# Running sums of an attention kernel: merge by transfer into two rings, numerators copied by VectorE, lent buffers placed by when they come free

## The chip, the cores and the metric

The kernel runs on one core of a Trainium2 chip. The metric is device time in microseconds (us), from the first to the last instruction of the core and what lies around it, as a median of several runs. Lower is better.

## The reference, cut to what matters

Two layers follow each other on an input of 4 x 256 x 48 x 48. Each normalizes its input in groups, computes and adds the result to the input. The first layer is a 3x3 convolution with batch norm and ReLU, then attention over all 2304 positions with 8 heads of 32 channels, then a projection. The second layer builds dynamic filters and a last batch norm. The change touches only the attention of the first layer:

```python
q, k, v = (qkv[:, :, :d], qkv[:, :, d:2 * d], qkv[:, :, 2 * d:])
attn = jax.nn.softmax(jnp.einsum('bhdn,bhdm->bhnm', q, k) * scale, axis=-1)
out = jnp.einsum('bhem,bhnm->bhen', v, attn).reshape(B, C, H, W)
out = jnp.einsum('oc,bchw->bohw', proj_w, out) + proj_b[None, :, None, None]
```

The kernel computes the softmax without subtracting the maximum: numerators (exponentials times v) and denominators (sums of exponentials over the keys) are built apart and divided at the end.

## The kernel before

The four batches run one after the other. For each, an attention stage (`attention`) is followed by a stage (`dynamic_filters`) that does the second layer of this batch, with the convolution and the q, k, v products of the next batch woven in by a planner that keeps a clock of estimated costs. The attention stage itself has no planner: its order is the order of the loop.

**Units and steps.** A unit is 512 queries of one group of four heads. Eight units cover 2048 queries of the two groups; the ninth (`last`) takes the remaining 256 queries of both groups. Each unit runs over 18 tiles of 128 keys, so a batch has 162 steps (u, m), in `steps`.

**One step.** `scores` issues the matmuls of the four heads (line 1331) into PSUM: head 0 into the tile `so` (one bank, one buffer), heads 1 to 3 into `se` (three banks, two buffers, which denominators and projections use as well, by `three`). ScalarE takes the exponentials (line 1339 for head 0, line 1340 for the rest) into a buffer `p` of 128 x 4 x 512 values, one of four that are used in rotation. One step later `weigh` multiplies p with v (line 1365) into the PSUM tile `num` (one buffer), and VectorE adds p to the running sum `acc` (line 1380).

**Lending.** From unit 1 on, at m = 2, 5, 8, 11 and 14 (`LENT`; the last unit leaves the fifth out), VectorE adds head 0 only. The other three heads are written by a transfer from GpSimd's queue into `extra`, a part of the weight ring: the first as a plain copy (line 1382), the others as accumulating transfers (line 1384). Each must wait for the one before it, because they accumulate in the same place. The buffer p is lent until the transfer has read it.

**End of a unit.** After m = 17, VectorE adds `extra` to `acc` (line 1387) and ScalarE copies the numerators from PSUM to `ao` (line 1390), which frees `num` for the next unit. The closing of the unit (`close`) comes later, at m = 1 of the unit after the next: matmuls with ones sum `acc` over the keys of a tile (line 1396), VectorE turns the result by two transposes and a reciprocal (lines 1408 to 1411) and multiplies the numerators (line 1418). In the last unit, unit 6 is closed at m = 1, unit 7 at m = 2, and the last itself at the end of the stage. There the sums over p, acc and extra are taken by matmuls alone.

**The last unit's two halves** share one `num` tile. To start it, four matmuls with a tile of zeros (line 1362) clear the bank ahead of the first products.

**Projections.** At m = 6 of units 3, 5, 7 and of the last unit one chunk (two in unit 7) of 384 columns is projected (`project`, line 1454) and added to the residual by VectorE (line 1463); SP stores it.

**The weight ring.** It has 3072 values per partition. `taken(t)` loads the weights of the next batch's convolution into it on SP's queue, a third at a time; `taken(0)` uses the last third. Before, `extra` is the first half of the ring, and `taken(0)` is issued ahead of the attention stage. `following[0]` (`opened`), called after the last step, starts the next convolution's sums on GpSimd and issues `taken(1)`.

Of the kernel before, what the change touches and what calls it, by code (L numbers as in the profile page):

```python
# [8 lines left out]
F32 = mybir.dt.float32  # L9
F32R = mybir.dt.float32r  # L10
AF = mybir.ActivationFunctionType
ALU = mybir.AluOpType
# [5 lines left out]
P = 128  # L18
NH = C // P
HEADS = 8  # L20
D = C // HEADS
# [4 lines left out]
NT = N // P  # L26
# [7 lines left out]
QC = 512  # L34
SAFE = 60.0
LENT = (2, 5, 8, 11, 14)
NEVER = float("inf")
LATE = (4, 3)
AHEAD = 2500.0
# [18 lines left out]
def conv_preact_kernel(  # L58
# [12 lines left out]
    nc = tc.nc  # L71
# [480 lines left out]
    with tc.tile_pool(name="w", bufs=1) as wpool, tc.tile_pool(  # L552
        name="act", bufs=1
# [14 lines left out]
        ring = wpool.tile([P, 3 * 1024], F32, tag="ring", name="ring")  # L568
# [735 lines left out]
        def attention(b, q, k_, vT, pools, spare, project, scratch, following):  # L1304


            ps_s, ps_a, work0 = pools
            ao = keep("h", f"ao_{b}")
            zeros = work0.tile([P, D], F32, tag="zeros", name=f"zeros_{b}", bufs=1)
            nc.gpsimd.memset(zeros, 0.0)  # L1310

            extra = scratch.rearrange("p (j n) -> p j n", j=3)
            scratch = work0.tile([P, QC], F32, tag="rt", name=f"rt_{b}", bufs=1)

            whole, rest = N // QC * QC, N % QC
            units = [[(g, q0, QC, 0)] for q0 in range(0, whole, QC) for g in range(NH)]
            units.append([(g, whole, rest, g * rest) for g in range(NH)])
            assert NH * rest == QC
            heads = [slice(j * D, (j + 1) * D) for j in range(4)]

            def three(name):
                return ps_s.tile([P, 3, 512], F32, tag="s", name=name)

            def scores(u, m):
                s1, s3 = ps_a.tile([P, 512], F32, tag="one", name=f"so_{b}_{u}_{m}"), three(f"se_{b}_{u}_{m}")
                for g, q0, n, at in units[u]:
                    for j, r in enumerate(heads):
                        dst = s3[:, j - 1] if j else s1  # L1330
                        nc.tensor.matmul(  # L1331
                            dst[:, at : at + n],
                            k_[r, g, m * P : (m + 1) * P],
                            q[r, g, q0 : q0 + n],
                            start=True,
                            stop=True,
                        )
                p = work0.tile([P, 4, QC], F32, tag="p", name=f"p_{b}_{u}_{m}", bufs=4)
                nc.scalar.activation(p[:, 0, :], s1, AF.Exp, scale=QS)  # L1339
                nc.scalar.activation(p[:, 1:, :], s3, AF.Exp, scale=QS)  # L1340
                return p

            state = {}
            last = len(units) - 1

            def weigh(u, m, p):
                if m == 0:
                    state[u] = dict(
                        num=ps_a.tile([P, 512], F32, tag="num", name=f"num_{b}_{u}"),
                        acc=work0.tile([P, 4, QC], F32, tag="acc", name=f"acc_{b}_{u}"),  # L1350
                    )
                st = state[u]
                several, end = len(units[u]) > 1, u == last
                if end and m >= NT - 2:
                    sums(u, p, m == NT - 2, m == NT - 1)
                    if m == NT - 2:
                        sums(u, st["acc"], False, False)
                        sums(u, extra, False, False, 1)
                if several and m == 0:

                    for j, r in enumerate(heads):
                        nc.tensor.matmul(st["num"][r, :], zeros, p[:, j, :], start=True, stop=False)
                for i, (g, q0, n, at) in enumerate(units[u]):
                    for j, r in enumerate(heads):
                        nc.tensor.matmul(  # L1365
                            st["num"][r, at : at + n],
                            vT[:, m, g * P + j * D : g * P + (j + 1) * D],
                            p[:, j, at : at + n],
                            start=(m == 0 and not several),
                            stop=(m == NT - 1 and i == len(units[u]) - 1),  # L1370
                        )
                if end and m >= NT - 2:
                    return
                if m == 0:
                    st["first"] = p
                else:
                    other = st["first"] if m == 1 else st["acc"]
                    lend = u > 0 and m in LENT[: len(LENT) - end]
                    js = slice(0, 1 if lend else 4)
                    nc.vector.tensor_tensor(st["acc"][:, js], other[:, js], p[:, js], ALU.add)  # L1380
                    if lend and m == LENT[0]:
                        nc.gpsimd.dma_start(out=extra, in_=p[:, 1:])  # L1382
                    elif lend:
                        nc.gpsimd.dma_start(out=extra, in_=p[:, 1:], accum_op=ALU.add)  # L1384
                if u and m == NT - 1 and not end:
                    rest = st["acc"][:, 1:]
                    nc.vector.tensor_tensor(rest, rest, extra, ALU.add)
                if m == NT - 1 and not end:
                    g, q0, n, _ = units[u][0]
                    nc.scalar.copy(ao[:, g, q0 : q0 + n], st["num"])  # L1390

            def sums(u, rhs, start, stop, first=0):
                if start:
                    state[u]["den"] = three(f"den_{b}_{u}")[:, 0, :]
                for j, r in enumerate(heads[first:]):
                    nc.tensor.matmul(
                        state[u]["den"][r, :], ones, rhs[:, j, :], start=start, stop=stop
                    )

            def close(u):  # L1400

                if u < last:
                    sums(u, state[u]["acc"], True, True)
                else:
                    busy(ps_a.tile([P, 512], F32, tag="one", name="warm"), 5)
                st = state.pop(u)
                t = scratch
                nc.vector.transpose(t, st["den"])
                rc = work0.tile([P, QC // D], F32, tag="rc", name=f"rc_{b}_{u}")
                nc.vector.reciprocal(rc, t.rearrange("p (k d) -> p k d", d=D)[:, :, 0])  # L1410
                nc.vector.transpose(
                    t.rearrange("p (k d) -> p k d", d=D),
                    rc.unsqueeze(2).to_broadcast([P, QC // D, D]),
                )
                for g, q0, n, at in units[u]:
                    dst = ao[:, g, q0 : q0 + n]
                    src = dst if u < last else st["num"][:, at : at + n]
                    nc.vector.tensor_tensor(dst, src, t[:, at : at + n], ALU.mult)

            steps = [(u, m) for u in range(len(units)) for m in range(NT)]  # L1420
            prev = None
            chunk = 0
            for i, (u, m) in enumerate(steps):
                ps = scores(u, m)


                if m == 1 and u > 1:
                    close(u - 2)
                if prev is not None:
                    weigh(*steps[i - 1], prev)  # L1430
                prev = ps
                if m == 2 and u == last:
                    close(u - 1)
                if m == 6 and (u % NH == 1 or u == last):
                    while (chunk + 1) * CH <= units[u if u == last else u - 1][0][1]:
                        pp = three(f"pp_{b}_{chunk}")
                        pp = [pp[:, o] for o in range(NH)]
                        if spare:
                            spare.pop(0)()
                        project(chunk, ao, pp)  # L1440
                        chunk += 1
            assert not spare
            weigh(*steps[-1], prev)
            following[0]()
            close(last)
            following[1]()
            return ao, chunk
# [918 lines left out]
        for b in range(B + 1):  # L2366
# [171 lines left out]
            if b == B - 1:  # L2538
# [1 line left out]
                    out=pads[B % 2].rearrange("p h r w -> p (h r w)")[:, : NH * (2 + NF) * CH],  # L2540
                    in_=late_d[0].rearrange("p m c -> p (m c)"),
                )
            scratch = ring[:, : 3 * QC]
            spare = []
            following = [lambda: None] * 2
            clear(pads[b % 2] if b else pads[1])
            if b + 1 < B:
                load_pad(b + 1)
                us[0] = taken(0)

                def opened(b=b):
                    coming.append(Blocks(b + 1, pads[(b + 1) % 2]))
                    coming[-1].stage0()
                    us[1] = taken(1)
# [97 lines left out]
```

## Time and profile before

| | |
|---|---|
| median of three runs | 2724.35 us (2721.27, 2724.35, 2724.39) |
| the profiled execution | 2722.09 us, of which the span is 2720.2 us |
| mean granted TensorE clock | 0.989 |
| busy: TensorE, VectorE, ScalarE, GpSimd | 2607.0, 2082.2, 1806.3, 809.3 us |
| exponentials, lines 1339 and 1340 | 648 each, 599 and 1449 ns |
| first to last start of line 1339, by batch | 152.4 to 516.6, 807.8 to 1175.6, 1470.0 to 1838.9, 2108.9 to 2477.3 us |
| running-sum adds, line 1380, on all four heads and on one | 412 of 2291 ns, 156 of 692 ns (36 first ones, 2285 ns) |
| merges, line 1387 | 28 of 1758 ns |
| numerator copies, line 1390 | 32 of 593 ns |
| lends, lines 1382 and 1384 | 32 and 124 |

A line of the profile names the source line, the engine, the operation, what it writes and reads, and the shape. In a timeline the first two columns are the start and the duration in us. Brackets at the end of a line give how long the engine had been idle and what ended that. TensorE appears twice: PE is the matmul, PEld the load of the stationary operand. Matmul ends are modelled, so start times are the safer reading. The time from one start of line 1339 to the next is one step of the attention stage.

### The profile page before, as it was taken

The page shows a single profiled execution, that of the slowest core. Times are in us where ns is not written, and L with a number is a line of the kernel's source. Part 1 is how long each engine was busy: PE and PEld are TensorE (multiplying, and loading weights), DVE is VectorE, ACT ScalarE, POOL GpSimd, SP SyncE. Part 2 cuts the span into 40 slices and gives each one's busy share as a digit, 9 for nine tenths or more (in the row PEclk, how much of TensorE's full clock was granted, in tenths as well). Part 3 has the DMA queues.
Part 4 walks back from the last instruction along what each step waited for, and adds up shares of the span by engine and source line. Part 5 has one row for each costly group of instructions (what it writes and reads, how often), then busy time and mean ns, then how long its engine had stood idle before and what let it go on. Part 6 is the DMA issues. An engine that isn't in the chain of part 4 may idle for free. (4 is left out here: it accounts for less than half of the span.)

```text
span 2720.2 us, 42536 instructions
## 1 busy us (share of the span) xinstructions
PE 2607.0 (96%) x16938; PEld 1102.1 (41%) x16938; DVE 2082.2 (77%) x2029; ACT 1806.3 (66%) x2287; POOL 809.3 (30%) x885
## 2 busy tenths in 40 slices
PE   6999999999999999999999999999989999999996
PEld 5632222555562222355555222245546222235554
DVE  7768888757739898857774988885775888885676
ACT  4479888734449898854445888884444888875344
POOL 5200100477520010067750000007775000100453
PEclk9999999999999999999999999999999999999998
DMA  4805445323252445423324354452324444432456
GB/s 174 223 13 105 108 98 110 90 60 108 65 104 58 99 95 108 99 74 87 94 63 84 76 105 99 94 111 75 84 73 120 107 100 99 99 88 72 121 165 219
DMA packets 136942, 273.67 MB, mean 101 GB/s; under 512 B 58024, under 2 KB 98384, under 8 KB 135712
## 3 DMA queue, kind: packets, MB, share of 16 engines
q0 software_dynamic: 26256, 137.71, 22.1%
q1 hardware_dynamic: 110480, 133.17, 18.3%
q8 instruction: 135, 2.21, 0.3%
q14 instruction: 71, 0.58, 0.1%
HBM read 112.12 MB, written 36.04 MB: 54 GB/s over the span
## 5 line engine op out<-in xcount | busy, mean ns | idle before, releaser
L1380 DVE TENSOR_TENSOR acc<-acc,p 128x2048 f32<-128x2048 f32 (+1 forms) x568 | 1052.0, 1852 | 121.0 <-ACT p L1340 71.6
L1340 ACT ACTIVATE p<-se 128x1536 f32<-128x1536 f32 x648 | 938.7, 1449 | 0.0
L1331 PE MATMUL so<-q,k 32*128 32x512 f32 (+1 forms) x1440 | 729.1, 594 | 18.5 <-ACT p L1339 15.9
L1331 PE MATMUL se<-q,k 32*128 32x512 f32 (+1 forms) x4320 | 737.8, 594 | 0.0
L1365 PE MATMUL num<-p,vT 128*32 128x512 f32 (+1 forms) x5760 | 711.9, 561 | 2.2 <-ACT ao L1390 2.2
L1339 ACT ACTIVATE p<-so 128x512 f32<-128x512 f32 x648 | 388.4, 599 | 195.2 <-PE se L1331 89.0
L1331 PEld LDWEIGHTS so<-q,k 32*128 32x128 f32 x1440 | 216.7, 183 | 535.6 <-ACT p L1339 492.0
L1834 POOL TENSOR_TENSOR near<-near,prod 128x384 f32<-128x384 f32 x352 | 353.3, 1037 | 255.3 <-DVE prod L1828 246.4
L1384 POOL DMA_DIRECT2D ring<-p x124 | 105.5, 851 | 776.4 <-ACT p L1340 481.4
L1365 PEld LDWEIGHTS num<-p,vT 128*32 128x32 f32 x5760 | 137.1, 108 | 480.2 <-issue 449.7
L1828 DVE TENSOR_TENSOR prod<-wb,pad 128x768 f32<-128x768 f32 x192 | 181.9, 953 | 84.6 <-ACT wb L1815 51.8
L1331 PEld LDWEIGHTS se<-q,k 32*128 32x128 f32 x4320 | 227.3, 183 | 5.1 <-ACT p L1340 4.1
L1815 ACT COPY wb<-ws 128x384 f32<-128x384 f32 x216 | 108.5, 506 | 166.0 <-DVE prod L1828 129.0
L1382 POOL DMA_DIRECT2D ring<-p x32 | 17.9, 559 | 632.2 <-ACT p L1340 485.1
L1992 PE MATMUL py<-far,wsc 128*128 128x384 f32 x512 | 169.9, 487 | 0.0
L1536 PE MATMUL pg<-pad,wcat 128*45 128x384 f32 x864 | 146.7, 490 | 8.5 <-ACT lg L1594 8.5
L1255 PE MATMUL pq<-hid,wqkv 128*128 128x384 f32 x384 | 133.1, 501 | 15.0 <-ACT hid L1125 12.8
L1504 ACT COPY far<-far 128x512 f32<-128x512 f32 x86 | 90.2, 1108 | 81.1 <-PE far L1762 77.8
L1992 PEld LDWEIGHTS py<-far,wsc 128*128 128x128 f32 x512 | 96.2, 190 | 66.0 <-issue 1.8
L1255 PEld LDWEIGHTS pq<-hid,wqkv 128*128 128x128 f32 x384 | 73.1, 194 | 69.2 <-ACT hid L1125 15.1
L1380 DVE TENSOR_TENSOR acc<-p,p 128x2048 f32<-128x2048 f32 x36 | 82.2, 2285 | 20.8 <-ACT p L1340 14.6
L1736 DVE COPY_PREDICATED amat<-along_y,bmat 128x768 f32<-128x768 uint32 x72 | 92.0, 1277 | 2.4
(334 smaller groups left out, 2865.1 us busy)
## 6 DMA issues: line engine op xcount, KB each, us to landing
ring<-p POOLq DMA_DIRECT2D x156, 768.0 KB, 5.7
ws<-w_d SPq DMA_DIRECT2D x216, 192.0 KB
ring<-u_d SPq DMA_DIRECT2D x36, 512.0 KB
pad<-in_x SPq DMA_DIRECT2D x14, 1152.0 KB
xst<-in_x POOLq DMA_DIRECT2D x36, 192.0 KB, 3.7
x_d<-pad SPq DMA_DIRECT2D x36, 192.0 KB
u_d<-pad SPq DMA_DIRECT2D x12, 512.0 KB
y_d<-y SPq DMA_DIRECT2D x13, 384.0 KB
```

The lines of the kernel that those rows point to most:

```text
L1255: nc.tensor.matmul(pq[:, :CH], wqkv[:, i, s, g * P : (g + 1) * P], hid[:, i, cols], start=(i == 0), stop=(i == NH - 1),)
L1331: nc.tensor.matmul(dst[:, at : at + n], k_[r, g, m * P : (m + 1) * P], q[r, g, q0 : q0 + n], start=True, stop=True,)
L1339: nc.scalar.activation(p[:, 0, :], s1, AF.Exp, scale=QS)
L1340: nc.scalar.activation(p[:, 1:, :], s3, AF.Exp, scale=QS)
L1365: nc.tensor.matmul(st["num"][r, at : at + n], vT[:, m, g * P + j * D : g * P + (j + 1) * D], p[:, j, at : at + n], start=(m == 0 and not s ...
L1380: nc.vector.tensor_tensor(st["acc"][:, js], other[:, js], p[:, js], ALU.add)
L1384: nc.gpsimd.dma_start(out=extra, in_=p[:, 1:], accum_op=ALU.add)
L1536: nc.tensor.matmul(pg[64 * s : 64 * s + NG, :CH], wcat[:, ii, k, :], shifted(ii, cc, k // 3 - 1, k % 3 - 1), start=(i == 0 and k == 0), st ...
L1815: nc.scalar.copy(pw[:, :CH], fetched[c, k][0])
L1828: nc.vector.tensor_tensor(prod.rearrange("p h (r w) -> p h r w", w=WW), wb, src, ALU.mult)
L1834: nc.gpsimd.tensor_tensor(cat[:, h], cat[:, h], prod[:, h], ALU.add)
L1992: nc.tensor.matmul(py[c][:, o, :CH], wsc[:, n * NH + i, o * P : (o + 1) * P], rhs, start=(n == 0 and i == 0), stop=(n == order[-1] and i = ...
```

## The change

1. **Numerators.** VectorE copies `num` to `ao` in place of ScalarE, for all units but the last. The copy is issued in `weigh` at m = 17, ahead of the running-sum add of that step.
2. **Two rings.** `extra` is now two halves of the weight ring, used by units in turn.
3. **Merge.** At the end of a unit an accumulating transfer from GpSimd's queue adds heads 1 to 3 of `acc` into `extra`, and the denominator matmuls read them there. Only unit 7 keeps VectorE's add.
4. **Unit 0 lends too**, at m = 9 and 14 (`FIRST`).
5. **Placement of p.** The four buffers are no longer used in rotation. Each step takes the buffer that is expected to be free first, where a lent buffer counts as held for 5 steps and another for 3 (`until`, `home`).
6. **Zero products** and the tile of zeros are gone: the first half of the last unit starts the bank, the second half does not.
7. **Moved:** in the last unit the closing of unit 7 from m = 2 to 4 and the projection from m = 6 to 8; `taken(0)` from ahead of the attention stage into `opened`, behind its last step.

```diff
 LENT = (2, 5, 8, 11, 14)
+FIRST = (9, 14)
...
-            zeros = work0.tile([P, D], F32, tag="zeros", name=f"zeros_{b}", bufs=1)
-            nc.gpsimd.memset(zeros, 0.0)
-
-            extra = scratch.rearrange("p (j n) -> p j n", j=3)
+
+            extra = scratch.rearrange("p (s j n) -> p s j n", s=2, j=3)
...
+            last = len(units) - 1
+            steps = [(u, m) for u in range(len(units)) for m in range(NT)]
+
+            def lends(u):
+                return FIRST if not u else LENT[:-1] if u == last else LENT
+
+            until, home = [0] * 4, {}
+            for i, (u, m) in enumerate(steps):
+                home[u, m] = until.index(min(until))
+                until[home[u, m]] = i + (5 if m in lends(u) else 3)
...
-                p = work0.tile([P, 4, QC], F32, tag="p", name=f"p_{b}_{u}_{m}", bufs=4)
+                p = work0.tile(
+                    [P, 4, QC], F32, tag=f"p{home[u, m]}", name=f"p_{b}_{u}_{m}", bufs=1
+                )
...
-                if several and m == 0:
-
-                    for j, r in enumerate(heads):
-                        nc.tensor.matmul(st["num"][r, :], zeros, p[:, j, :], start=True, stop=False)
...
-                            start=(m == 0 and not several),
+                            start=(m == 0 and i == 0),
...
+                if m == NT - 1:
+                    g, q0, n, _ = units[u][0]
+                    nc.vector.tensor_copy(ao[:, g, q0 : q0 + n], st["num"])
...
-                    lend = u > 0 and m in LENT[: len(LENT) - end]
+                    lend = m in lends(u)
...
-                    if lend and m == LENT[0]:
-                        nc.gpsimd.dma_start(out=extra, in_=p[:, 1:])
+                    if lend and m == lends(u)[0]:
+                        nc.gpsimd.dma_start(out=extra[:, u % 2], in_=p[:, 1:])
                     elif lend:
-                        nc.gpsimd.dma_start(out=extra, in_=p[:, 1:], accum_op=ALU.add)
-                if u and m == NT - 1 and not end:
+                        nc.gpsimd.dma_start(
+                            out=extra[:, u % 2], in_=p[:, 1:], accum_op=ALU.add
+                        )
+                if m == NT - 1 and not end:
                     rest = st["acc"][:, 1:]
-                    nc.vector.tensor_tensor(rest, rest, extra, ALU.add)
-                if m == NT - 1 and not end:
-                    g, q0, n, _ = units[u][0]
-                    nc.scalar.copy(ao[:, g, q0 : q0 + n], st["num"])
+                    if u == last - 1:
+                        nc.vector.tensor_tensor(rest, rest, extra[:, u % 2], ALU.add)
+                    else:
+                        nc.gpsimd.dma_start(out=extra[:, u % 2], in_=rest, accum_op=ALU.add)
+                        rest = extra[:, u % 2]
+                    st["parts"] = [st["acc"][:, 0], *(rest[:, j] for j in range(3))]
...
-                    sums(u, state[u]["acc"], True, True)
+                    sums(u, state[u]["parts"], True, True)
...
-                if m == 2 and u == last:
+                if m == 4 and u == last:
                     close(u - 1)
-                if m == 6 and (u % NH == 1 or u == last):
+                if m == (8 if u == last else 6) and (u % NH == 1 or u == last):
...
-            scratch = ring[:, : 3 * QC]
+            scratch = ring[:, : 6 * QC]
...
-                us[0] = taken(0)

                 def opened(b=b):
+                    us[0] = taken(0)
                     coming.append(Blocks(b + 1, pads[(b + 1) % 2]))
```

More of the change, by code (lines that the diff above doesn't have):

```diff
@@ L1343, in attention @@
             state = {}
-            last = len(units) - 1
             def weigh(u, m, p):
@@ L1352, in weigh @@
                 st = state[u]
-                several, end = len(units[u]) > 1, u == last
+                end = u == last
                 if end and m >= NT - 2:
@@ L1357, in weigh @@
                         sums(u, st["acc"], False, False)
-                        sums(u, extra, False, False, 1)
-                if several and m == 0:
-                    for j, r in enumerate(heads):
-                        nc.tensor.matmul(st["num"][r, :], zeros, p[:, j, :], start=True, stop=False)
+                        sums(u, extra[:, u % 2], False, False, 1)
                 for i, (g, q0, n, at) in enumerate(units[u]):
@@ L1396, in sums @@
                     nc.tensor.matmul(
-                        state[u]["den"][r, :], ones, rhs[:, j, :], start=start, stop=stop
+                        state[u]["den"][r, :], ones, rhs[j] if type(rhs) is list else rhs[:, j],
+                        start=start, stop=stop,
                     )
@@ L1418, in close @@
                     nc.vector.tensor_tensor(dst, src, t[:, at : at + n], ALU.mult)
-            steps = [(u, m) for u in range(len(units)) for m in range(NT)]
             prev = None
```

## The prediction

> **What bounds the kernel now.** I read first the table of waits, then timelines. The edits lie in the attention stage, and there the exponentials (ScalarE, lines 1339 and 1340) and the matmuls (TensorE, lines 1331 and 1365) run in turn. The waits of the former (total us, times, longest):
>
> ```profile
> ACT p L1339 <- PE se L1331: 89.0, 163, 5.5
> ACT p L1339 <- DMA ring<-p: 23.9, 25, 2.3
> ACT p L1339 <- DVE acc L1380: 10.9, 22, 1.5
> ```
>
> A quiet step on TensorE (start, duration; each product is issued twice, so scores and numerators are two passes each):
>
> ```profile
> 240.15 1.07 PE L1365 MATMUL num<-p,vT 128*32 128x512 f32 x8
> 241.15 0.69 PE L1331 MATMUL so<-q,k 32*128 32x512 f32 x1
> ...
> 241.68 0.59 PE L1331 MATMUL so<-q,k 32*128 32x512 f32 x1
> ...
> 242.22 1.07 PE L1365 MATMUL num<-p,vT 128*32 128x512 f32 x8
> ```
>
> 242.22 − 240.15 = 2.07 us, with no gap; ScalarE, right after a stall, does a step in 1.82 (411.38 to 413.20). So TensorE sets the floor: 18 steps are 37.26 us per unit. Above it lie stalls. The first kind, on ScalarE:
>
> ```profile
> 408.99 1.45 ACT L1340 ACTIVATE p<-se 128x1536 f32<-128x1536 f32 x1
> 411.38 0.60 ACT L1339 ACTIVATE p<-so 128x512 f32<-128x512 f32 x1 [0.95 <-DMA ring<-p]
> ...
> 415.52 0.60 ACT L1339 ACTIVATE p<-so 128x512 f32<-128x512 f32 x1 [0.37 <-PE se L1331]
> ```
>
> The buffer that the exponential wants, four steps after it was lent, is still being read by the transfer. The wait for TensorE two steps later is its echo, so the 23.9 us above is not the full price. The second kind stands at each change of unit:
>
> ```profile
> 390.62 0.60 ACT L1339 ACTIVATE p<-so 128x512 f32<-128x512 f32 x1 [0.46 <-DMA ring<-p]
> ...
> 392.44 0.59 ACT L1390 COPY ao<-num 128x512 f32<-128x512 f32 x1
> 392.90 0.63 ACT L1339 ACTIVATE p<-so 128x512 f32<-128x512 f32 x1
> 395.62 0.60 ACT L1339 ACTIVATE p<-so 128x512 f32<-128x512 f32 x1 [0.74 <-PE so L1331]
> 398.15 0.60 ACT L1339 ACTIVATE p<-so 128x512 f32<-128x512 f32 x1 [0.57 <-PE se L1331]
> ```
>
> ```profile
> 393.08 0.13 PEld L1365 LDWEIGHTS num<-p,vT 128*32 128x32 f32 x4 [0.32 <-ACT ao L1390]
> ...
> 394.93 0.30 PEld L1331 LDWEIGHTS se<-q,k 32*128 32x128 f32 x6 [0.18 <-ACT p L1340]
> ```
>
> Three steps take 398.15 − 390.62 = 7.53 instead of 6.21: the copy pushes the second exponential back, and the scores behind it wait for that exponential's bank.
>
> I add up the starts of line 1339, unit by unit (first start to the next unit's first start). Units 0 to 7 of the four batches sum to 321.9, 326.8, 327.9 and 325.9 us. A quiet unit from the third on is 37.26 + 1.33; units 3 and 5 carry one projection (+2.79: the step of 2.07 becomes 4.86), unit 7 two (+5.36).
>
> **What the Trainium skill says.** "TensorEngine Tiling (Array Packing)", Key Properties: a change of tiling mode drains the array. The trace agrees: scores are 32*128, numerators 128*32, and the weight loads idle 0.76 us ahead of each switch. This is why 2.07 is a floor that no edit here lowers. "VectorE: DVE Perf Modes", Why PSUM operands drop a tier: VectorE has one read port into PSUM, so an f32 copy from there runs at the base rate. The trace has such a copy of the same size, which is my price:
>
> ```profile
> L1506 DVE COPY xT<-xa x4: 690/691/692, 543.1 to 2499.6; 128x512 f32<-128x512 f32 x4
> ```
>
> "SBUF — State Buffer", Who interferes with whom: a VectorE copy in a two-port mode locks GpSimd out and delays the transfers that GpSimd issues. By the VectorE page a copy out of PSUM can't be in that mode, so I charge nothing to the lends; no run here shows it.
>
> **The change, part by part.** Times are from a unit's first exponential, S0.
>
> Numerator copy to VectorE: 32 × 0.593 = 19.0 us leave ScalarE, 32 × 0.69 = 22.1 reach VectorE. There the copy stands ahead of the last running-sum add. The add before it ends near S0 + 0.4, the numerators near S0 + 0.9 (a pass of 1.07 that starts 0.17 ahead of S0 when no lend stalls it), so it runs from 1.0 to 1.7. TensorE wants that bank at about 2.9 (behind the four denominator matmuls), or at 2.0 in unit 1, which has none: hidden, by 1.2 and 0.3. If the copy came behind the 2.29 us add instead, it would end at 4.0 and cost 1 to 2 us a unit. With ScalarE free, the second exponential ends at 3.92, not 4.3, and the scores that waited for it start at 3.97: the fourth exponential at 7.13 instead of 7.54. Gain 0.41 a boundary; the denominator's 0.92 stays. Units 2 to 7, four batches: 24 × 0.41 = **9.8 us**.
>
> Lent buffers placed by need: following the rule for `home`, a lent buffer is wanted again after 5 or 6 steps, no longer 4. An accumulating lend takes 5.7 to 7.4 us from issue:
>
> ```profile
> DMA to landing us min/median/max: 5.7/5.8/7.4
> ```
>
> Lent at m = 5, it is issued near S0 + 13.4 and lands by 20.8 at worst; the buffer is wanted at 21.6. Those with 6 steps have 2 us more. So the stalls go. Their price, with echoes, is what units 2 to 7 take (245.7, 249.3, 250.7, 247.1 in the four batches) over their quiet length (3 × 38.59 + 2 × 41.38 + 43.95 = 242.5): 3.2 + 6.9 + 8.2 + 4.6 = **22.9 us**. In turn other buffers come round after 3 steps, 72 times a batch. Then the add must end within about 4.2 us of its exponential: its own 2.29 leaves 1.9 for VectorE's lag. Between lends the lag is at most 2 × (2.29 − 2.07) = 0.44; worst is m = 6 behind a projection, with 0.65 us to spare in units 5 and 7. Charged: nothing.
>
> Unit 0 lends twice: 8 adds shrink from 2.29 to 0.69, 12.8 us off VectorE. It now ends unit 0 in lag (17 × 0.22 = 3.7 us), which shows in unit 1's steps of 2.4. Unit 1 takes 38.8, 39.9, 39.4 and 39.2; without lag, copy and lend stalls it has no excess over 37.26: **8.2 us**, and 0.5 at the end of unit 0.
>
> Merge by transfer: 28 adds of 1.76 us (line 1387) become 4, 42.2 us off VectorE; 28 accumulating transfers join GpSimd's queue. Each waits there for the last add (S0 + 4.0) and the landing of m = 14 (about S0 + 1), and lands by 11.4. Behind it in the queue stands only m = 2 of the next unit, ready at 7.1 and written to the other ring, so not held; it may share the DMA engines (lends take 3.5 alone; I allow 3 more), and its buffer is wanted at 17.5. The denominator reads the ring a unit later. Price nothing on the path; if transfers doubled, m = 5 would start late and its margin of 0.8 would be lost, a few us in all.
>
> Last unit: 16 zero matmuls go (1.06 us a batch), with their four memsets on GpSimd, which nothing waited for. But VectorE has copy, add, kept merge (1.76), the closing (2.4) and the next add in a row: to 10.4, when the fifth exponential (nominal 9.2) wants the buffer. With the later closing a second wait of 0.3 to 0.5 follows at the eighth. I get the tenth exponential at 25.0 against 24.4 before: −0.6 × 4. The moved projection is neutral. Lend stalls of 1.2 and 1.4 in batches 0 and 3 go: net **+0.3**.
>
> The first weight load of the next batch moves on SP's queue from ahead of attention to its end, behind the stores of x1. It waits for the upper ring, last read in unit 7. The convolution starts 13 us after the last exponential (529.73 against 516.58), held by GpSimd: hidden; uncovered it would be at most 3 × 5 us.
>
> Sum: 9.8 + 22.9 + 8.2 + 0.5 + 0.3 = 41.7 us. From the profiled execution's 2722.09 (span 2720.2, 1.9 around it) that gives 2680.4; it lies 2.3 below the median of 2724.35, so for a median I say **2681**. What is late next is TensorE at 2.07 a step.
>
> **Rivals.** (A) As summed: 2681, between 2672 and 2690; chance 0.62. (B) Half of it: the transfers slow each other or VectorE's lag bites at the 3-step buffers, and only boundaries and half of the stalls come back, some 21 us: 2703. For it: lends already chain, each waiting for the one before (266 us of GpSimd's waits); against it: the 5 to 6 steps. Chance 0.2. (C) More: TensorE fell to half clock in one attention stall (0.54 granted at 1664.5 to 1666.5); fewer idle gaps could spare others outside my units: 2667, chance 0.1. (D) The time is given back after attention, GpSimd's chain holding the next stage: 2722; against it, that chain starts at the last scores and moves with them. Chance 0.03. (E) Slower: the 3-step buffers. If VectorE were so late that each of the 288 reuses held the exponential for over 42/288 = 0.15 us, the gain is gone; at 0.2 us it is 2724 − 42 + 58 = 2740. It needs a lag above 2.1 us where I find 0.44, so 0.05.
>
> **How the numbers follow.** The measurement can tell about 0.2% (5.4 us) from no change. Faster is A, B and C: 0.92; same is D: 0.03; slower is E: 0.05. The range runs from C's edge to B: 2667 to 2703.
>
> **What would show it.** In the profile after: lend waits ahead of the first exponential near zero, and none on VectorE's adds; boundary steps of about 2.0, 3.05, 2.1; units of 37.3, 38.2, 41.0, 43.5; transfers still at 5.7. Wrong if adds end the exponentials' waits in mid-unit (E), if the numerators wait for VectorE's copy, or if lends land over 8 us after issue (B).

## The result, and the profile after

| | before | after |
|---|---|---|
| median of four runs each | 2722.81 us (2718.02 to 2724.39) | 2690.59 us (2688.79 to 2697.66) |
| ratio, 95% interval | | 0.9882 (0.9868 to 0.9897) |
| the profiled execution; its span | 2722.09; 2720.2 us | 2697.66; 2695.8 us |
| busy: VectorE, ScalarE, GpSimd | 2082.2, 1806.3, 809.3 us | 2048.7, 1795.7, 833.1 us |
| attention, first to last start of head 0's exponentials, four batches | 1469.4 us | 1433.6 us |
| all the rest of the span | 1250.8 us | 1262.2 us |

The kernel is 32 us faster; the forecast was 41.7 (2681), with a range of 2667 to 2703. The attention stage gave 1469.4 − 1433.6 = 35.8 us. By the unit lengths (first start of head 0's exponential to that of the next unit; the last unit to its last start), summed over the batches:

| units | before | after | gained | forecast |
|---|---|---|---|---|
| 2 to 7 | 992.8 | 963.3 | 29.5 | 22.9 + 9.8 = 32.7 |
| 1 | 157.3 | 150.3 | 7.0 | 8.2 |
| 0 | 152.4 | 153.1 | −0.7 | 0.5 |
| last | 166.9 | 167.0 | −0.1 | 0.3 |

From the table of waits after the change (total us, times, longest): what the accumulating lends (line 1391) still wait for each other, 266.1 us before, and the exponentials' waits for scores. The exponentials' waits for a transfer (23.9 us before) are gone from the table, and those for VectorE's adds (10.9 us before) are down to 7.2:

```profile
POOL ring L1391 <- DMA ring<-p: 111.8, 19, 6.9
...
ACT p L1348 <- PE se L1338: 53.5, 55, 5.5
...
ACT p L1348 <- PE so L1338: 36.1, 39, 1.9
```

That nothing of the transfers is left ahead of an exponential is shown by the view of line 1348 alone (now the exponential of head 0), which lists all that ended its engine's idle time (us, times):

```profile
its engine sat idle before it (us, times) until:
  PE se L1338: 53.5, 55
  PE so L1338: 36.1, 39
  DVE acc L1387: 7.2, 8
  issue: 2.4, 1
```

The 7.2 us of VectorE come 8 times, twice a batch, all in the last unit. The change of unit on ScalarE, with S0 = 388.44 as the unit's first exponential:

```profile
388.44 0.60 ACT L1348 ACTIVATE p<-so 128x512 f32<-128x512 f32 x1
...
390.51 0.60 ACT L1348 ACTIVATE p<-so 128x512 f32<-128x512 f32 x1
391.01 1.44 ACT L1349 ACTIVATE p<-se 128x1536 f32<-128x1536 f32 x1
393.44 0.60 ACT L1348 ACTIVATE p<-so 128x512 f32<-128x512 f32 x1 [0.99 <-PE so L1338]
...
395.72 0.60 ACT L1348 ACTIVATE p<-so 128x512 f32<-128x512 f32 x1 [0.34 <-PE se L1338]
...
397.79 0.60 ACT L1348 ACTIVATE p<-so 128x512 f32<-128x512 f32 x1
```

The steps are 2.07, 2.93, 2.28 and 2.07: three steps take 395.72 − 388.44 = 7.28 us, where before they took 7.53 and the forecast had 7.13. VectorE at the same place:

```profile
389.49 0.69 DVE L1380 COPY ao<-num 128x512 f32<-128x512 f32 x1 [0.59 <-PE num L1369]
390.10 2.28 DVE L1387 TENSOR_TENSOR acc<-acc,p 128x2048 f32<-128x2048 f32 x1
```

The copy runs from 1.05 to 1.74 us after S0, as forecast (1.0 to 1.7), and the add ends at 3.94 (4.0). TensorE's timeline shows the pass that needs the copied bank, and the scores that wait for the second exponential:

```profile
391.31 1.04 PE L1369 MATMUL num<-p,vT 128*32 128x512 f32 x8
392.29 0.69 PE L1338 MATMUL so<-q,k 32*128 32x512 f32 x1
392.51 0.70 PE L1338 MATMUL se<-q,k 32*128 32x512 f32 x3
```

391.31 is S0 + 2.87 (forecast 2.9), 1.13 us behind the copy's end. The new transfers (line 1399) land as the old ones did:

```profile
DMA to landing us min/median/max: 5.7/5.8/7.0
```

### The profile page after: what moved, and what is told of

Same layout as the page of the kernel before. It is cut to its first block, busy times and chain, and to the rows that moved or that the text cites. A ratio compares the mean times of both kernels' runs of the same rounds, so it can differ in the third digit from the quotient of the medians.

```text
span 2695.8 us, 42480 instructions
## 1 busy us (share of the span) xinstructions
PE 2593.6 (96%) x16906; PEld 1095.7 (41%) x16906; DVE 2048.7 (76%) x2037; ACT 1795.7 (67%) x2255; POOL 833.1 (31%) x917
## 5 line engine op out<-in xcount | busy, mean ns | idle before, releaser
L1387 DVE TENSOR_TENSOR acc<-acc,p 128x2048 f32<-128x2048 f32 (+1 forms) x568 | 1039.0, 1829 | 107.1 <-ACT p L1349 60.0
L1369 PE MATMUL num<-p,vT 128*32 128x512 f32 (+1 forms) x5760 | 700.9, 561 | 1.1 <-DVE ao L1380 0.9
L1391 POOL DMA_DIRECT2D ring<-p x128 | 108.8, 850 | 813.2 <-ACT p L1349 526.6
L1369 PEld LDWEIGHTS num<-p,vT 128*32 128x32 f32 x5760 | 129.0, 108 | 476.5 <-issue 457.5
L1389 POOL DMA_DIRECT2D ring<-p x36 | 20.1, 559 | 312.9 <-ACT p L1349 156.0
L1399 POOL DMA_DIRECT2D ring<-acc x28 | 23.9, 853 | 237.3 <-DVE acc L1387 237.3
```

Source lines behind the costliest of these rows:

```text
L1369: nc.tensor.matmul(st["num"][r, at : at + n], vT[:, m, g * P + j * D : g * P + (j + 1) * D], p[:, j, at : at + n], start=(m == 0 and i == ...
L1391: nc.gpsimd.dma_start(out=extra[:, u % 2], in_=p[:, 1:], accum_op=ALU.add)
```

## The experiments

All ratios are to the kernel before, on the same chip in turn. "Attention" is the sum over four batches from the profiled execution (before 1469.4, after 1433.6).

| run | median us (lowest to highest) | ratio (95%) | attention us |
|---|---|---|---|
| after_again | 2684.68 (2682.18 to 2695.36) | 0.988 (0.986 to 0.9899) | 1431.6 |
| rotate | 2713.26 (2711.57 to 2715.35) | 0.9975 (0.9964 to 0.9985) | 1461.3 |
| act_copy | 2691.02 (2688.63 to 2693.13) | 0.9895 (0.988 to 0.991) | 1435.4 |
| dve_merge | 2711.23 (2706.45 to 2713.74) | 0.9964 (0.995 to 0.9978) | 1458.8 |
| place_only | 2694.34 (2691.14 to 2696.9) | 0.9891 (0.9873 to 0.9908) | 1440.6 |
| no_first | 2706.24 (2702.56 to 2710.82) | 0.9941 (0.9924 to 0.9958) | 1449.8 |
| last_merge | 2679.6 (2673.51 to 2685.57) | 0.9838 (0.9817 to 0.9858) | 1427.0 |
| last_late | 2686.68 (2682.71 to 2688.85) | 0.9868 (0.9848 to 0.9888) | 1427.3 |
| zeros_back | 2686.41 (2684.62 to 2693.51) | 0.9881 (0.9861 to 0.9902) | 1431.5 |
| last_old | 2688.18 (2686.25 to 2691.48) | 0.9886 (0.9869 to 0.9902) | 1433.3 |
| last_best | 2684.28 (2677.56 to 2687.91) | 0.9872 (0.9855 to 0.9888) | 1426.8 |
| light_exp | 2678.56 (one run) | | 1422.9 |

My theory was that the placement brings most, that the copy by VectorE adds a fixed piece at each change of unit, and that merge and unit 0's lends pay for the room that this takes on VectorE. The rival: that less work on VectorE and ScalarE is what brings the gain, whatever the placement.

**after_again: the changed kernel a second time.** No edit.

> The changed kernel once more, as the base for the other three on the same chip. Expected 2690 us (2686 to 2695), ratio 0.988. Units 2 to 7 keep 38.3, 41.1 and 43.7 us from first exponential to first exponential whatever the run; if the time differs from the other executions by several us, the difference lies in the granted clock of the other stages, not in these units.

The median is 2684.68; the profiled execution took 2683.11, against 2697.66 for the one above. Their attention stages differ by 2.0 us, the rest by 1262.2 − 1249.8 = 12.4. The granted clock differs too. The first line is the kernel after, the second this run (span, mean granted TensorE clock):

```profile
core 0: 2695.8 us, clock 0.985
```

```profile
core 0: 2681.3 us, clock 0.992
```

By the record of the clock, TensorE was at half of it for 80.3 us in the first, 43.6 in the second and 58.9 in the kernel before. So the 1262.2 of the first table is no cost of the change: the same kernel's rest takes 1249.8 here, one less than before. About half of the 12.4 us lies between the first and the second attention stage, where the first profile took 297.8 us with 17.1 of them at half clock and this one 291.4 with 3.4.

**rotate: the buffers rotate again, all else as after.**

```diff
-                    [P, 4, QC], F32, tag=f"p{home[u, m]}", name=f"p_{b}_{u}_{m}", bufs=1
+                    [P, 4, QC], F32, tag="p", name=f"p_{b}_{u}_{m}", bufs=4
```

> The changed kernel with its four p buffers in rotation again, so that a lent one is wanted after four steps; all else as changed. Theory (the wait for a lent buffer cost some 23 us in units 2 to 7 and a few in unit 1): 2690 + 22 to 28 = 2712 to 2718 us, with lend transfers named again ahead of the exponentials in mid-unit. Rival (the two rings and the relief of VectorE removed those stalls, the placement adds little): 2690 to 2696 us.

28.6 us slower than after_again, 29.7 of it in attention. In the table of waits the lends are back ahead of the exponentials, more of them than before the change (23.9 us, 25 times). With them come the echoes: waits for TensorE's scores in `se` 147 times, where the changed kernel has 55:

```profile
ACT p L1348 <- PE se L1338: 72.9, 147, 5.5
...
ACT p L1348 <- DMA ring<-p: 34.8, 41, 2.1
```

So the rival falls: with all that moves work off VectorE and ScalarE, but without the placement, a gain of 0.25% is left.

**place_only: the kernel before, with the placement alone.**

```diff
-                p = work0.tile([P, 4, QC], F32, tag="p", name=f"p_{b}_{u}_{m}", bufs=4)
+                p = work0.tile([P, 4, QC], F32, tag=f"p{home[u, m]}", name=f"p_{b}_{u}_{m}", bufs=1)
```

with `home` computed as in the change, but with unit 0 lending nothing.

> The kernel before with the placement of the p buffers alone (one ring, merge by VectorE, copy by ScalarE, unit 0 lends nothing, zero products kept). Theory (lend stalls were 22.9 us in units 2 to 7, 2.7 in the last unit and some 3 in unit 1): 2723 - 23 to 28 = 2695 to 2700 us, with no lend transfer named ahead of an exponential. Rival (without the second ring the lends still chain and hold the exponentials): within 5 us of 2723.

Attention fell by 1469.4 − 1440.6 = 28.8 us, of the whole change's 35.8. The view of its exponentials (line 1346 here) has no transfer either:

```profile
  PE se L1338: 63.7, 64
  PE so L1338: 25.7, 32
  DVE acc L1387: 7.0, 16
  issue: 3.1, 1
```

Units 2 to 7 gave 992.8 − 970.5 = 22.3 (one of the 24 was 1.1 us longer than its like, 39.67 against 38.57), unit 1 3.9 and the last 3.2. The other parts together add 7.2 in units 2 to 7 and 3.1 in unit 1, and take 3.3 back in the last. The two medians, 2694.34 here and 2690.59 or 2684.68 for the whole, can hardly be told apart by their ratios; the unit lengths can be.

**act_copy: after, with the numerators copied by ScalarE.**

```diff
-                    nc.vector.tensor_copy(ao[:, g, q0 : q0 + n], st["num"])
+                    nc.scalar.copy(ao[:, g, q0 : q0 + n], st["num"])
```

> The changed kernel with the numerators copied by ScalarE again; all else as changed. Theory (the copy delays the second exponential of a unit and with it the scores behind it): 0.3 to 0.4 us at each of 28 boundaries, 2690 + 8 to 12 = 2698 to 2702 us, the third and fourth exponentials later as in the kernel before. Rival (ScalarE has slack, VectorE has less): 2688 to 2691 us.

Too much was expected: attention is only 1.8 to 3.8 us longer than in the two profiles of the changed kernel. The lengths say why. Units 2 to 7 take 38.57, 41.35 and 43.93, each 0.25 more than after (38.32, 41.10, 43.68). But the last unit takes 40.64 where after it takes 41.74, so the copy on VectorE costs 1.1 there. 24 × 0.25 = 6.0 and 0.6 in unit 1 (37.73 a batch) stand against 4 × 1.1 = 4.4, which leaves 2.2. So all but about 2 to 4 us of the change's gain in attention stays without VectorE's copy. In units 2 to 7 the lengths are those of place_only to within 0.01 (its two longer units apart), although the merge goes by transfer here and by VectorE there: while ScalarE copies, taking the merge off VectorE brings nothing in these units. The boundary on ScalarE, with the copy back:

```profile
390.07 0.60 ACT L1348 ACTIVATE p<-so 128x512 f32<-128x512 f32 x1
...
391.89 0.59 ACT L1380 COPY ao<-num 128x512 f32<-128x512 f32 x1
392.36 0.63 ACT L1348 ACTIVATE p<-so 128x512 f32<-128x512 f32 x1
...
395.07 0.60 ACT L1348 ACTIVATE p<-so 128x512 f32<-128x512 f32 x1 [0.74 <-PE so L1338]
...
397.60 0.60 ACT L1348 ACTIVATE p<-so 128x512 f32<-128x512 f32 x1 [0.58 <-PE se L1338]
```

397.60 − 390.07 = 7.53, as in the kernel before, against 7.28.

**dve_merge: after, with VectorE's merge in every unit.**

```diff
-                    if u == last - 1:
+                    if True:
```

> The changed kernel with the merge done by VectorE in every unit (the 1.76 us add comes back in units 0 to 6); all else as changed. Theory (at a boundary VectorE has the copy, an add, the closing and the next add in a row, which ends at about 8.6 us where the fifth exponential wants the buffer at 9.35; with 1.76 more it ends at 10.4): about 1.0 us lost in each of units 2 to 7 and little in unit 1, 2690 + 24 to 30 = 2714 to 2720 us, with a wait of the exponential for VectorE's add. Rival (the merge was off the path, as it was in the kernel before): 2688 to 2693 us.

26.6 us slower than after_again (2711.23 to 2684.68), 25.2 to 27.2 of it in attention: each of units 2 to 7 is 1.06 longer (39.38, 42.15, 44.74). VectorE has no slack left behind its copy. Its timeline, and then ScalarE's fifth exponential:

```profile
396.39 1.76 DVE L1397 TENSOR_TENSOR acc<-acc,ring 128x1536 f32<-128x1536 f32 x1
...
400.45 2.29 DVE L1387 TENSOR_TENSOR acc<-p,p 128x2048 f32<-128x2048 f32 x1
402.84 11.07 DVE L1387 TENSOR_TENSOR acc<-acc,p 128x512 f32<-128x512 f32 x6
```

```profile
402.83 0.60 ACT L1348 ACTIVATE p<-so 128x512 f32<-128x512 f32 x1 [1.19 <-DVE acc L1387]
```

The fifth exponential starts when the first add of the unit ends, after ScalarE has stood idle for 1.19 us. So the merge by transfer is needed once VectorE copies: place_only has the same merge on VectorE, with the copy on ScalarE, and its units 2 to 7 are as long as act_copy's.

**no_first: after, unit 0 lends nothing and merges nothing.**

```diff
-FIRST = (9, 14)
+FIRST = ()
...
-                    if u == last - 1:
+                    if u == 0:
+                        pass
+                    elif u == last - 1:
```

> The changed kernel, but unit 0 lends nothing and needs no merge. Theory (unit 0 leaves VectorE 3.7 us behind, and the copy now stands in that queue ahead of the next unit's numerators): 6 to 9 us more than the changed kernel, 2696 to 2699 us, lost in the first six steps of unit 1 and at the end of unit 0. Rival (the lag is absorbed by the four buffers): 2689 to 2692 us.

The place is right, the size is not: unit 1 takes 168.1 in the four batches against 150.3, 17.8 us more (43.12, 40.62, 42.20, 42.20). In batch 0, VectorE's adds of unit 0 run on without a gap into unit 1 (S0 = 189.37), and the copy is queued behind one of them. VectorE, then TensorE:

```profile
182.20 11.88 DVE L1387 TENSOR_TENSOR acc<-acc,p 128x2048 f32<-128x2048 f32 x5
193.99 0.69 DVE L1380 COPY ao<-num 128x512 f32<-128x512 f32 x1
```

```profile
190.72 0.59 PE L1338 MATMUL so<-q,k 32*128 32x512 f32 x1
...
194.73 1.94 PE L1369 MATMUL num<-p,vT 128*32 128x512 f32 x8 [3.40 <-DVE ao L1380]
196.59 1.22 PE L1338 MATMUL so<-q,k 32*128 32x512 f32 x1
```

TensorE stands for 3.40 us, and then its matmuls take about twice as long. Two windows within the gap and two after it (window, length, busy time and count of TensorE, weight loads, VectorE, ScalarE and GpSimd, granted clock, DMA share, GB/s):

```profile
191.30:193.20 1.90, 0.03 (x4) 0.00 (x0) 1.80 (x2) 1.44 (x3) 0.00 (x0) 1.00 0.00 0
193.30:194.70 1.40, 0.00 (x0) 0.00 (x0) 1.40 (x3) 0.41 (x1) 0.00 (x0) 0.50 0.00 0
...
198.10:200.00 1.90, 1.90 (x12) 0.20 (x8) 1.64 (x2) 1.30 (x2) 0.00 (x0) 0.50 0.00 0
200.10:204.00 3.90, 3.90 (x36) 0.94 (x32) 0.56 (x1) 2.95 (x4) 0.53 (x1) 1.00 0.50 201
```

The clock fell from 1.00 to 0.50 at 193.25, within the gap, and rose again at 200.07: 6.83 us at half clock, of which TensorE worked for the last 5.3. The Trainium skill says in "TensorE: Matmul & The Clock Gate", What's actually happening, that TensorE falls to half its clock after an idle window of about 3.4 us and needs about as long a busy one to rise again. The trace agrees in part: the stretch at half clock is two times 3.41 us long, but the clock fell 1.9 us after the last matmul, not 3.4.

Half clock is only a part of the loss. In the same unit batches 2 and 3 have 3.41 us of it and batch 1 has none; there unit 1 is shortest, and its 40.62 is still 3.1 over the changed kernel's 37.56. By my estimate from this batch some 12 of the 17.8 us are the wait itself.

**zeros_back: after, with the zero products** (and their tile) of before.

```diff
+                if end and m == 0:
+                    for j, r in enumerate(heads):
+                        nc.tensor.matmul(st["num"][r, :], zeros, p[:, j, :], start=True, stop=False)
...
-                            start=(m == 0 and i == 0),
+                            start=(m == 0 and not end),
```

> The changed kernel with the four zero products of the last unit back. Theory (VectorE's chain sets the last unit's first steps, so that TensorE has room there): the last unit takes 41.7 to 42.0 us in place of 41.74, no change in time. Rival (the products stand on TensorE's path): 42.8 us, 4 us more in all.

The last unit takes 41.74, as it does after; attention is 1431.5, after_again's is 1431.6. Its second step is 0.86 us longer (3.80 against 2.94), but the fifth exponential, which waits for VectorE, starts at S0 + 10.41 in both. So TensorE isn't what is late there; what the products cost once VectorE holds nothing was not tried.

**last_old: after, with the closing and the projection of the last unit where they were.**

```diff
-                if m == 4 and u == last:
+                if m == 2 and u == last:
...
-                if m == (8 if u == last else 6) and (u % NH == 1 or u == last):
+                if m == (6 if u == last else 6) and (u % NH == 1 or u == last):
```

> The changed kernel with unit 7 closed at m = 2 and the chunk projected at m = 6 of the last unit, as in the kernel before. Theory (VectorE has the same work in the same few steps, so the place changes little): the last unit takes 41.4 to 42.3 us in place of 41.74. Rival (the move spared a double closing): over 43 us, 5 us more in all.

41.99 against 41.74 in each batch: moving them was worth 1.0 us in all.

**last_merge: after, with unit 7 merged by transfer too.**

```diff
-                    if u == last - 1:
-                        nc.vector.tensor_tensor(rest, rest, extra[:, u % 2], ALU.add)
-                    else:
-                        nc.gpsimd.dma_start(out=extra[:, u % 2], in_=rest, accum_op=ALU.add)
-                        rest = extra[:, u % 2]
+                    nc.gpsimd.dma_start(out=extra[:, u % 2], in_=rest, accum_op=ALU.add)
+                    rest = extra[:, u % 2]
```

> The changed kernel with unit 7 merged by transfer too, so that VectorE's 1.76 us add at the start of the last unit goes. Theory (the last unit's waits of 1.2 us at the fifth and 0.6 us at the eighth exponential end at VectorE's chain): the last unit takes 40.3 to 40.7 us in place of 41.74, 4 to 6 us less in all, 2684 to 2687 us. Rival (the closing's matmuls on TensorE set it): no change, 2690.

What it cures stands in the timelines of the changed kernel's last unit, VectorE first, then the fifth and the eighth exponential on ScalarE:

```profile
471.49 0.69 DVE L1380 COPY ao<-num 128x512 f32<-128x512 f32 x1 [0.60 <-PE num L1369]
472.10 2.28 DVE L1387 TENSOR_TENSOR acc<-acc,p 128x2048 f32<-128x2048 f32 x1
474.41 1.76 DVE L1397 TENSOR_TENSOR acc<-acc,ring 128x1536 f32<-128x1536 f32 x1
...
478.48 2.28 DVE L1387 TENSOR_TENSOR acc<-p,p 128x2048 f32<-128x2048 f32 x1
```

```profile
480.85 0.60 ACT L1348 ACTIVATE p<-so 128x512 f32<-128x512 f32 x1 [1.18 <-DVE acc L1387]
...
488.64 0.60 ACT L1348 ACTIVATE p<-so 128x512 f32<-128x512 f32 x1 [0.62 <-DVE acc L1387]
```

The last unit went from 41.74 to 40.22 in each batch: 4 × 1.52 = 6.1 us. The view of line 1348 in this run has no VectorE left:

```profile
its engine sat idle before it (us, times) until:
  PE se L1338: 52.7, 59
  PE so L1338: 35.4, 35
  issue: 3.0, 1
```

Its interval, 0.9817 to 0.9858, lies below both of the changed kernel's. The two runs that follow hold the same edit and the same attention within 0.3 us, and gave 2686.68 and 2684.28; so I count on the 6 us of the unit lengths, not on all that its median shows.

**last_late: last_merge, with unit 7 closed at m = 7 and projected at m = 10.**

```diff
-                if m == 4 and u == last:
+                if m == 7 and u == last:
...
-                if m == (8 if u == last else 6) and (u % NH == 1 or u == last):
+                if m == (10 if u == last else 6) and (u % NH == 1 or u == last):
```

> As the one before it, and unit 7 is closed at m = 7 of the last unit in place of 4, the projection at m = 10 in place of 8, where the buffers that come next have four steps. Theory: VectorE's lag is spread, the last unit takes 39.2 to 39.8 us, 2681 to 2684 us. Rival (the closing costs the same wherever it stands): as the one before.

The theory fell: 40.29, not shorter than 40.22. The closing has only moved: in last_merge its steps are the fifth and sixth (3.00 and 2.23 us), here the eighth and ninth (2.94 and 2.29), 5.23 us both times. It costs the same wherever it stands.

**last_best: last_merge, with ScalarE copying unit 7's numerators.**

```diff
-                    nc.vector.tensor_copy(ao[:, g, q0 : q0 + n], st["num"])
+                    (nc.scalar.copy if u == last - 1 else nc.vector.tensor_copy)(ao[:, g, q0 : q0 + n], st["num"])
```

> Unit 7 merged by transfer and its numerators copied by ScalarE, the other units as changed. Theory (VectorE's chain at the start of the last unit gets 0.69 us shorter, ScalarE's boundary 0.25 us longer): the last unit takes 39.7 to 40.0 us against 40.22 with the merge alone, 1 to 2 us less in all, within the noise of the time, about 2680 us. Rival: 40.2 or more.

The theory fell here as well: 40.47, 0.25 more than last_merge. Once the merge is gone VectorE no longer holds the last unit, and ScalarE's copy costs its 0.25 as at every other change of unit. So the 1.1 that the copy on VectorE costs in the changed kernel is a cost of copy and merge in a row, not of the copy.

**light_exp: after, without the exponentials of the fourth head** (ScalarE's second activation takes two heads). The four buffers are made once per batch, with the fourth head's part set to one.

```diff
-                nc.scalar.activation(p[:, 1:, :], s3, AF.Exp, scale=QS)
+                nc.scalar.activation(p[:, 1:3, :], s3[:, :2], AF.Exp, scale=QS)
```

> The changed kernel without the exponentials of the fourth head of each group: that part of the four buffers is set to one once per batch, so ScalarE's second activation takes about 1.0 us in place of 1.45; TensorE's and VectorE's work is the same. Theory (TensorE's four passes and two changes of mode are the floor of a step): quiet steps stay at 2.07 us. Rival (ScalarE's 1.9 us, or the loop of exponential and scores through ScalarE, sets it): 1.6 to 1.8 us.

A quiet stretch on ScalarE:

```profile
240.21 0.60 ACT L1352 ACTIVATE p<-so 128x512 f32<-128x512 f32 x1 [0.56 <-PE se L1344]
240.70 1.02 ACT L1353 ACTIVATE p<-se 128x1024 f32<-128x1024 f32 x1
242.28 0.60 ACT L1352 ACTIVATE p<-so 128x512 f32<-128x512 f32 x1 [0.56 <-PE se L1344]
```

The second activation takes 1.02 in place of 1.45, and the step is 2.07 still; ScalarE now waits 0.56 us for the scores. So the second activation does not set the step, and TensorE does, as the prediction read it. At the change of unit the steps became 2.07, 2.92 and 2.07: of the 1.07 us by which the changed kernel's three steps (7.28) exceed three quiet ones, ScalarE's second activation makes about 0.2.

## Why the prediction was right, and where it was off

The mechanism was right, and the sum of 41.7 was 5.9 too high against the 35.8 of attention: 3.2 in units 2 to 7, 1.2 in unit 1, 1.2 in unit 0 and 0.4 in the last (rounded). The 1.2 of unit 0 is scatter, as shown below; by after_again's profile attention gave 1469.4 − 1431.6 = 37.8.

- **Lent buffers, 22.9 us.** Measured alone, by place_only: 22.3 in units 2 to 7. Undone alone, by rotate: 29.7 in the whole of attention. The reading "quiet length against measured length", which counts the echoes and not the waits of 23.9 us alone, was exact to a few per cent. The 5 or 6 steps were enough: no lend is waited for, although an accumulating one landed only after 7.6 us and a plain one after 7.9.
- **3-step buffers, charged at nothing.** Right: in units 2 to 7 of the changed kernel no exponential waits for an add. Rival E (slower) and rival B (half of it) both needed such waits or transfers that land later than 8 us; neither came.
- **The copy, 0.41 a boundary.** This is the term that was mis-sized: it measured 0.25 (act_copy against after, and 7.53 to 7.28 in the timelines). The prediction let the second exponential end at S0 + 3.92 and the scores behind it start at 3.97. Measured: the exponential starts at 391.01 and ends at 392.45, S0 + 4.01, and the scores start at 392.51, S0 + 4.07. ScalarE's first step can't be shorter than TensorE's 2.07, which the prediction itself gave as the floor; it took 2.0, from a unit whose S0 had been held by a lend, so that the scores for the second exponential were ahead of it. What the fourth exponential loses is 7.28 − 7.13 = 0.15 each time, 24 × 0.15 = 3.6 us, about the 3.2 that units 2 to 7 lack. (29.5 is then 24 × 0.25 = 6.0 for the copy and 23.5 for the stalls.)
- **The copy's place on VectorE.** Right in units 2 to 7: it lies between 1.05 and 1.74 and its bank is wanted at 2.87. In unit 1 it was wrong (next point). The Trainium skill, "SBUF — State Buffer", Who interferes with whom, was the reason to look at GpSimd's transfers beside such a copy. The accumulating lends kept their median of 5.8 us, but this does not test the point: none of the 32 copies ran while GpSimd executed an instruction of a transfer; the 13 lends in flight beside a copy had been issued at least 3.37 us ahead of it.
- **Unit 0's lends and unit 1, 8.2 us.** Unit 1 gained 7.0 and stands at 37.42, 37.56, 37.92 and 37.41, not 37.26. Here one of the prediction's own signs of being wrong came true: the numerators wait for VectorE's copy. It was to end at 1.7 with the bank wanted at 2.0; it starts only at 1.41 to 1.92 after S0 and ends at 2.09 to 2.61, so VectorE is still late from unit 0, and the second steps of the four batches take 1.3 us more than 2.07 each. That is about the whole shortfall of 1.2. The lends of unit 0 are worth far more once the copy is on VectorE (17.8 us, no_first), which the prediction did not see. It took them for a gain of their own. They are that too: with the copy on ScalarE unit 1 takes 37.73 in act_copy and 38.35 in place_only, whose unit 0 lends nothing. But above all they are a condition of the copy.
- **Merge by transfer, nothing on the path.** The transfers cost nothing, as forecast. Without VectorE's copy they bring nothing in units 2 to 7 either (act_copy beside place_only); that they have to go with the copy is shown by dve_merge (1.06 a unit).
- **The last unit, 0.3 gained.** −0.1 measured, with the same steps as forecast: the fifth exponential waits 1.18 for VectorE, the eighth 0.62 (forecast 0.3 to 0.5). Zero products: nothing while VectorE is late (zeros_back). Moved closing and projection: 0.25 a batch (last_old); the forecast had the move of the projection as neutral. Lend stalls gone: 1.2 and 1.4 in batches 0 and 3, as forecast (42.30 and 42.48 before, 41.06 in the other two; place_only has 40.93 in all four).
- **Unit 0, 0.5 gained.** −0.7 in the first profile, where unit 0 of batch 0 took 38.62 at a mean granted clock of 0.96; in after_again it took 37.24 at 1.00, and unit 0 gained 152.4 − 151.0 = 1.4. In batches 1 and 2, equal in both profiles (37.34), it gained 0.15 and 0.50. So the sign of the forecast was right.
- **Nothing is given back outside attention** (rival D): 1249.8 us in after_again against 1250.8. That half clock alone makes up the 12.4 us by which the two profiles of the changed kernel differ there is not shown: in rotate the rest takes 1249.6 us with 58.4 of them at half clock, in after_again 1249.8 with 38.5.
- **TensorE's floor of 2.07.** Right as a number: quiet steps take it in every run, in light_exp too. Why it is 2.07 is not shown. The prediction reads the weight loads' 0.76 us of idle time ahead of each switch as the drain of the array. The profile has 0.76 only ahead of the numerators; ahead of the scores it is 0.84, ended by line 1339's exponential, and the matmuls themselves have no gap at a switch.

So the parts aren't a sum. The placement brings 28.8 us of attention by itself. All else together brings 7.0 more. Most of that does not need the copy: act_copy, with all but the copy, has 1435.4, which is 5.2 below place_only. The copy by itself adds 1.8 to 3.8, and only with the merge by transfer and unit 0's lends beside it: without one or the other attention takes 1458.8 (dve_merge) or 1449.8 (no_first), both over place_only's 1440.6.

## What to carry to other kernels

Where a buffer goes out on loan to a transfer, count in how many steps of the loop it is wanted again and place the loans by that; price the stall by the length of the stage against its quiet length, since each wait has an echo. When work moves to an engine with little slack, price it with everything that stands in a row with it at that place: the same copy was worth 0.25 us at a change of unit, cost 1.1 us in the last unit or held TensorE for 3.4 us, according to what was queued around it. And when a stall goes, the step falls back to the floor of the next engine and no lower: don't take a shorter one from a place that had been stalled.

## What the hardware showed that was not expected

- In one gap of 3.40 us on TensorE in the middle of a busy stage the granted clock fell to 0.50, 1.9 us after the last matmul, and stayed there for 6.83 us; a pass of scores took 1.22 us in place of 0.69. In all profiles of this case a stretch at half clock that ends before the span does is 3.41, 6.83 or 10.24 us long.
- Executions of the changed kernel differ by some 15 us (2682.18 to 2697.66), and in the two that were profiled TensorE was at half clock for 43.6 and 80.3 us. For a change of a few us the length of the units says more than the time of the whole.
- The plain lend (line 1389) landed 3.5 us after its issue at best, 4.8 in the median and 7.9 at worst; before (line 1382) it was 3.5, 3.5 and 4.8. 28 of the 36 now have a merge of the unit before in flight beside them, and all but one of these take 4.4 us or more; of the other eight none takes over 3.9. The accumulating ones stayed between 5.7 and 7.6.
